# Layer 3's cross-attention values: worked out at layer 2's end instead of beside layer 0's experts

## The chip, the cores and the metric

The kernel runs on one core of a Trainium2 chip. The core has a matrix engine (TensorE, in profiles PE, with its weight loads as PEld), a vector engine (DVE), a scalar engine (ACT), GpSimd (POOL) and a queue processor (SP) that issues most DMAs. Each takes its instructions strictly in order; they meet through semaphores. The metric is the device time of one execution in microseconds, as a median of several.

## The reference, cut to what matters

Four decoder layers, each an attention, a cross-attention to a short context (4 batches of 77 tokens of 128 numbers) and a feed-forward block. The change touches only the preparation of layer 3's cross-attention, whose keys and values come from the context alone:

```
def _L3_xattn_ref(query, key, value, w_q, w_k, w_v, w_o):      # key = value = ctx_1024
    q = (query @ w_q).reshape(B, Q, HEADS, HEAD_DIM).transpose(0, 2, 1, 3)   # 16 heads of 64
    k = (key @ w_k).reshape(B, Kl, HEADS, HEAD_DIM).transpose(0, 2, 1, 3)
    v = (value @ w_v).reshape(B, Kl, HEADS, HEAD_DIM).transpose(0, 2, 1, 3)
    attn = jax.nn.softmax(jnp.einsum('bhqd,bhkd->bhqk', q, k) * scale, axis=-1)
    out = jnp.einsum('bhqk,bhkd->bhqd', attn, v)
    return out.transpose(0, 2, 1, 3).reshape(B, Q, HEADS * HEAD_DIM) @ w_o
...
x = x + _L2_ffn_ref(_layernorm(x), ...)
x = x + _L3_attn_ref(_layernorm(x), Wq, Wk, Wv)     # softmax over the batch axis, then a causal mask
x = x + _L3_xattn_ref(_layernorm(x), ctx_1024, ctx_1024, w_q, w_k, w_v, w_o)
```

Since `attn @ (v_h @ w_o_h)` equals `(attn @ v_h) @ w_o_h`, the kernel multiplies each head's values with its rows of `w_o` ahead of time: a table of 16 heads x 77 tokens x 4 batches x 128 numbers, called `vo`.

## The kernel before, in words

**Tiling.** Activations lie as x, 16 tiles of 128 tokens by 128 numbers (4 tiles a batch), and transposed as xT (128 by 2048). Everything is in float32. A matmul of 128 by 128 weights with 512 columns appears in the profile as two records. Matmul results go to eight banks of PSUM, which are dealt out under tags: `f`, `acc` and `s` while expert blocks run, `mm` (7) and `s` (1) from layer 2's feed-forward block to the end of layer 3's attention.

**Order.** The program is written as Python generators. `weave(dense, chain, every, lead)` takes steps of a dense stream and puts a step of a chain in after every `every` steps; `turns` alternates streams. A scheduler then orders each engine's instructions by that priority and by what it reckons to be ready. On the chip the order is fixed: an instruction that waits holds up all behind it on its engine.

**Stage A (345 to 472 us).** The dense stream is `ffn("l0_ffn", second, ...)`, layer 0's experts for batches 2 and 3 (two matmuls gate and up into banks `f`, an activation on ACT at L1029, one product with up and one with the routing weight c on DVE, a down matmul into `acc` at L1037), in turns with `l3_context`. The chain is layer 1's attention and cross-attention for batches 0 and 1 and the routing of layer 1's experts (`route`): two norms, transposes (L516), the context softmax (POOL's reduction, L536, turned at L543), the sigmoid (L585), the choice of 8 experts on DVE, the turned weights (L666), a store of these to DRAM and the load of c (L989). The next weave has layer 1's experts as its dense stream: two shared units a batch that need no c, then routed ones that do. At most five units can wait for c (tile `h` has five buffers, `f` four banks).

`l3_context` (L2079) runs over eight head pairs hp. For each: a matmul for keys (weights w_k, 128 columns) and a copy `x3kT` by ACT, stored to DRAM (`x3_k`); a matmul for values (w_v) and a copy `x3vT`; after a yield, eight matmuls of 77 rows with w_o (two heads, four batches), two copies `x3vo` by ACT and one store to DRAM (`x3_vo`).

**Stage B (1878 to 1980 us).** Layer 2's feed-forward ends with `l2_dense(b)` for each batch (residual, norm, two dense matmuls through bank `s`, norm, and the layer's closing norm). `l3_keys` then fills `kb` and `vo` from DRAM: a memset by POOL and loads by SP. Beside `dense(3)` runs layer 3's attention: `project(b)` (q, k, v of a batch), `three()` (scores and exps of the first three batches), then `project(3)` and `fourth()` (the last batch's scores, the rescaling of all four on DVE and POOL) and `close(b)`. `l3_xattn` comes after it; it reads `kb` from its second step and `vo` in its step `values`, from 1991 us on.

**Weights.** `want(i)` loads packs of the list `feed` into four slots in turn; `pack` returns them. A load waits until the slot's earlier weights are used up. `load` takes a pack into a pool of its own.

Of the kernel before, what the change touches and what calls it, by code (L numbers as in the profile page):

```python
# [13 lines left out]
F32 = mybir.dt.float32  # L14
# [8 lines left out]
P = 128  # L23
B, S, D = 4, 512, 128
NT = B * S // P
TB = S // P
L = 77
# [264 lines left out]
class Net:  # L292
# [1786 lines left out]
    def l3_context(self, pool):  # L2079

        nc = self.nc
        Wk, Wv, Wo = (self.load("l3_xattn." + n, pool, "x3" + n) for n in "kvo")
        kd = self.away.tile([2, 64, 8, B, L], F32, name="x3_k")
        vd = self.away.tile([16 * L, B, D], F32, name="x3_vo")
        self.x3 = kd, vd
        yield
        for hp in range(8):
            c = slice(hp * P, hp * P + P)
            pk = self.bank("f", (P, B, L))
            self.dot(pk.rearrange("p b l -> p (b l)"), (Wk["k"][:, c], self.const["ctxT"]))  # L2090
            k = pool.tile([P, B, L], F32, tag="x3kT", name="x3kT", bufs=2)
            nc.scalar.copy(k, pk)
            for h in range(2):
                nc.sync.dma_start(kd[h, :, hp], k[64 * h : 64 * h + 64])
            pv = self.bank("f", (P, B * L))
            self.dot(pv, (Wv["v"][:, c], self.const["ctxT"]))
            vT = pool.tile([P, B * L], F32, tag="x3vT", name="x3vT", bufs=2)
            nc.scalar.copy(vT, pv)
            yield
            vo = pool.tile([L, 2, B, D], F32, tag="x3vo", name="x3vo", bufs=2)  # L2100
            for h in range(2):
                po = self.bank("f", (P, B, D))
                r = slice(64 * h, 64 * h + 64)
                for b in range(B):
                    self.dot(po[:L, b, :], (vT[r, b * L : b * L + L], Wo["o"][r, c]))
                nc.scalar.copy(vo[:, h], po[:L])
            nc.sync.dma_start(vd[2 * hp * L : 2 * (hp + 1) * L].rearrange("(h l) b d -> l h b d", l=L), vo)
            yield

    def l3_keys(self, pool):  # L2110


        kd, vd = self.x3
        kb = pool.tile([P, 8, B, 2, L], F32, name="kb")
        n, rest = 16 * L // P, 16 * L % P
        vo = pool.tile([P, n + 1, B, D], F32, name="vo")
        self.nc.gpsimd.memset(kb, 0.0)
        for h in range(2):
            self.nc.sync.dma_start(kb[64 * h : 64 * h + 64, :, :, h, :], kd[h])
        self.nc.sync.dma_start(vo[:, :n], vd[: n * P].rearrange("(r p) b d -> p r b d", p=P))  # L2120
        self.nc.sync.dma_start(vo[:rest, n], vd[n * P :])
        self.x3 = kb, vo

    def l3_xattn(self, base, pool):

# [78 lines left out]
def chained(*chains):  # L2204
    for c in chains:
        yield from c


def some(steps, n):

    for _ in range(n):
        if next(steps, steps) is steps:
            return
        yield


def build(nc, packs, dram):
    first, second = GROUPS
    of = lambda stage: [n for n in packs if n.startswith(stage + ".") and n[-1].isdigit()]
    f2 = [f"l2_ffn.{kind}{hp}" for hp in range(8) for kind in ("qkv", "o")]  # L2220
    feed = ["l0_attn.qk", "l0_attn.vo"]
    at = {}
    for name, part in (
        ("l0a", of("l0_ffn")), ("l0b", of("l0_ffn")), ("l1a", of("l1_ffn")), ("l1b", of("l1_ffn")),
        ("l2", f2 + f2), ("x3", ["l3_xattn.q"]), ("l3", of("l3_ffn")[:3]),
    ):
        at[name] = len(feed)
        feed += part
    with tile.TileContext(nc) as tc, ExitStack() as ctx:
        net = Net(ctx, tc, packs, dram, feed)  # L2230
# [3 lines left out]
        def open_pool(name, right=False):  # L2234
            pools[name] = ExitStack()
            return pools[name].enter_context(net.pool(name, right=right))

        close_pool = lambda name: pools.pop(name).close()
# [31 lines left out]
        s2 = open_pool("s2", right=True)  # L2270
        w2 = net.load("s2", s2, "w")

        def chain2(group):
            yield from both(group, lambda b: chained(net.l1_attn(b, w2, s2), net.l1_xattn(b, w2, s2)))
            yield from net.route("l1_ffn", group, w2, s2)
# [1 line left out]
        x3c = open_pool("x3c")  # L2277
        net.weave(
            net.turns(net.ffn("l0_ffn", second, 16, at["l0b"], ff), net.l3_context(x3c)),
            chained(net.l1_context(s2, w2), chain2(first)), 0.48, 3,  # L2280
        )
        close_pool("x3c")
        net.weave(net.ffn("l1_ffn", first, 64, at["l1a"], ff), chain2(second), 0.97, 3)
# [26 lines left out]
        f2 = open_pool("f2")  # L2310
# [15 lines left out]
        dense = lambda b, fast=False: net.l2_dense(b, y[b], w4, s4, fast)  # L2326
# [2 lines left out]
        close_pool("f2")  # L2329


        net.l3_keys(open_pool("x3c"))
        a3 = open_pool("a3")
        net.want(at["x3"])
        project, three, fourth, close = net.l3_attn(w4, a3)
        net.weave(dense(3, fast=True), chained(project(0), project(1), project(2), three()), 1.15)
        net.weave(chained(project(3), fourth()))
        net.weave(chained(*[close(b) for b in range(B)]), net.norm(0), 1, 1)
        close_pool("a3")
        close_pool("s4")  # L2340
        close_pool("gates")

# [2 lines left out]
        x3 = open_pool("x3")  # L2345
# [38 lines left out]
        dense = net.ffn("l3_ffn", (3,), 32, at["l3"], ff, net.spread3)  # L2384
# [31 lines left out]
```

## Time and profile before

| what | value |
|---|---|
| median of 4 runs | 2236.36 us (2231.95 to 2237.71) |
| profiled execution: device time, span | 2243.5 us, 2241.7 us |
| PE busy | 2102.8 us (94%), 8980 matmul records |
| DVE, ACT, POOL busy | 1606.3 (72%), 998.2 (45%), 555.6 us (25%) |
| first and last `x3vo` copy (ACT) | 349.9 and 446.7 us, 16 copies of 0.58 us |
| `vo` loads issued | 1874.1 and 1883.6 us (2304 and 160 KB) |
| first and last read of `vo` (L2189) | 1991.0 and 2122.6 us |
| mean DMA rate | 96 GB/s |

The profile is of one execution, which ran 7 us above the median; sums against its rows are made against its own span. Busy times of PE are those of pipelined records and overlap by up to 0.17 us at each change of group, so start times are the better measure of what a matmul costs. "Idle before" names the engine and line whose signal ended a wait. Granted clock is TensorE's, 1.00 at full speed.

### The profile page before, as it was taken

Reading aid. Unit: us, or ns where it says so; the run is one execution under the profiler, and the core shown is the slowest. Engines: PE = TensorE matmul, PEld = TensorE weight load, DVE = VectorE, ACT = ScalarE, POOL = GpSimd, SP = SyncE. Lnnn points to the kernel's source line nnn. Section 1 sums busy time; section 2 is a strip of 40 time slices with the busy share of each in tenths; the row PEclk is TensorE's granted clock in tenths of the full one; section 3 lists DMA queues with packets and bytes.
Section 4 is the critical chain, followed back from the end, with each engine's and each line's share of the span. In section 5 each row is a group of like instructions: output and inputs, shape, how many; then the busy total and the mean of one; then the engine's idle time right before and its main releaser. Section 6 shows DMA issues by size and latency. Waiting matters only on the chain.

```text
span 2241.7 us, 28186 instructions
## 1 busy us (share of the span) xinstructions
PE 2102.8 (94%) x8980; PEld 1114.1 (50%) x8980; DVE 1606.3 (72%) x4061; ACT 998.2 (45%) x2044; POOL 555.6 (25%) x695
## 2 busy tenths in 40 slices
PE   6999899999999999899999999999999999499887
PEld 3556555645544554445444544444444444366553
DVE  7676576476675768778977788776776774688735
ACT  4565545543434554434543454343433344356531
POOL 1000000000000000433333333333333331335733
PEclk8998899999999999999999999999999999799988
DMA  6321144154344342333443444443444344111122
GB/s 169 94 72 44 34 115 121 61 127 117 104 129 113 84 122 78 104 85 101 106 116 96 106 117 120 122 120 105 115 112 107 94 112 102 57 39 34 31 73 78
DMA packets 89811, 214.93 MB, mean 96 GB/s; under 512 B 21970, under 2 KB 40850, under 8 KB 89406
## 3 DMA queue, kind: packets, MB, share of 16 engines
q1 hardware_dynamic: 86094, 209.20, 35.0%
q0 software_dynamic: 3568, 3.93, 0.6%
q8 instruction: 71, 1.16, 0.2%
q14 instruction: 78, 0.64, 0.1%
HBM read 184.00 MB, written 23.53 MB: 93 GB/s over the span
## 4 chain that ended last, share of the span: by engine, by line
PE 73%; DVE 16%; issue 4%; ACT 3%; POOL 2%; DMA 1%; SPq 0%; another core or an unknown queue 0%; DVEq 0%; POOLq 0%; ACTq 0%
PE mm L426 20%; PE f L426 13%; PE mm L1878 8%; PE s L426 8%; PE acc L1037 6%; PE mm L1850 5%; PE mm L1825 4%; DVE h L437 2%; PE mm L1160 1%; PE mm L1227 1%; DVE m L1167 1%; PE mm L1205 1%; DVE at_m L1907 1%; PE acc L2189 1%; PE s L516 1%
## 5 line engine op out<-in xcount | busy, mean ns | idle before, releaser
L1786 POOL TENSOR_TENSOR gvx<-gvx 128x512 f32<-128x512 f32 (+1 forms) x256 | 260.4, 1017 | 551.2 <-DVE gvx L437 482.7
L426 PE MATMUL f<-xT,w_l_ffn 128*128 128x512 f32 (+1 forms) x700 | 338.1, 605 | 1.2 <-ACT h L1029 0.7
L1909 ACT ACTIVATE at_e<-mm,at_m 128x512 f32<-128x512 f32 x256 | 173.0, 685 | 294.2 <-DVE at_m L1907 275.5
L426 PE MATMUL mm<-w_l_ffn_qkv,xT 128*128 128x512 f32 x512 | 267.0, 606 | 4.2 <-ACT at_e L1909 1.7
L1878 PE MATMUL mm<-og,w_l_ffn_o 128*128 128x512 f32 x512 | 265.2, 602 | 1.4 <-DVE og L437 1.4
L437 DVE TENSOR_TENSOR h<-h,f 128x512 f32<-128x512 f32 (+1 forms) x192 | 131.1, 684 | 142.8 <-PE f L426 103.7
L1029 ACT ACTIVATE h<-f 128x512 f32<-128x512 f32 x189 | 112.4, 596 | 240.4 <-PE f L426 200.4
L1037 PE MATMUL acc<-h,w_l_ffn 128*128 128x512 f32 x378 | 196.7, 604 | 6.8 <-DVE h L437 6.2
L426 PEld LDWEIGHTS f<-xT,w_l_ffn 128*128 128x128 f32 (+1 forms) x700 | 126.9, 192 | 132.9 <-issue 112.0
L437 DVE TENSOR_TENSOR gvx<-mm,gv 128x512 f32<-128x512 f32 x256 | 174.5, 683 | 22.4 <-PE mm L426 18.6
L437 DVE TENSOR_TENSOR og<-mm,c 128x512 f32<-128x512 f32 x256 | 173.9, 681 | 18.3 <-PE mm L1878 16.1
L1826 ACT COPY eT<-mm 128x512 f32<-128x512 f32 x256 | 137.6, 596 | 83.4 <-PE mm L1825 83.2
L1907 DVE TENSOR_REDUCE at_m<-mm 128x1 f32<-128x512 f32 x256 | 161.0, 681 | 11.9 <-PE mm L426 10.5
L1825 PEld LDWEIGHTS mm<-ident,at_e 128*128 128x128 f32 x1024 | 120.8, 142 | 68.1 <-issue 47.6
L1878 PEld LDWEIGHTS mm<-og,w_l_ffn_o 128*128 128x128 f32 x512 | 91.8, 191 | 112.2 <-issue 91.0
L1825 PE MATMUL mm<-ident,at_e 128*128 128x128 f32 x1024 | 136.2, 275 | 5.3 <-ACT at_e L1909 5.3
L426 PEld LDWEIGHTS mm<-w_l_ffn_qkv,xT 128*128 128x128 f32 x512 | 87.6, 191 | 95.1 <-issue 59.0
L426 PE MATMUL mm<-roped 64*128 64x512 f32 x512 | 130.9, 622 | 1.7 <-DVE roped L437 1.1
L1167 DVE TENSOR_REDUCE m<-mm 128x1 f32<-128x512 f32 (+3 forms) x176 | 104.9, 635 | 34.9 <-PE mm L1163 34.0
L1850 PE MATMUL mm<-eT,v 128*64 128x512 f32 x512 | 118.6, 599 | 0.0
L1037 PEld LDWEIGHTS acc<-h,w_l_ffn 128*128 128x128 f32 x378 | 70.9, 192 | 91.8 <-issue 61.6
L437 DVE TENSOR_TENSOR h<-h,c 128x512 f32<-128x512 f32 x160 | 110.4, 695 | 3.7 <-DMA c<-l_ffn_w 0.9
(458 smaller groups left out, 3557.1 us busy)
## 6 DMA issues: line engine op xcount, KB each, us to landing
c<-gates SPq DMA_DIRECT2D x256, 256.0 KB
c<-l_ffn_w SPq DMA_DIRECT2D x96, 384.0 KB
w_l_ffn<-in_l_ffn SPq DMA_DIRECT2D x26, 576.0 KB
w_l_ffn_qkv<-in_l_ffn_qkv SPq DMA_DIRECT2D x16, 640.0 KB
w_l_ffn_o<-in_l_ffn_o SPq DMA_DIRECT2D x16, 512.0 KB
rot<-qk SPq DMA_DIRECT2D x128, 64.0 KB
d<-inverted SPq DMA_DIRECT2D x64, 128.0 KB
k_parts<-k SPq DMA_DIRECT2D x12, 384.0 KB
```

Of the source, the lines that this page charges most:

```text
L426: self.nc.tensor.matmul(out, lhsT=lhsT, rhs=rhs, start=i == 0, stop=i == len(pairs) - 1)
L437: self.nc.vector.tensor_tensor(out, a, b, op)
L1029: nc.scalar.activation(h, pg, AF.Silu)
L1037: nc.tensor.matmul(acc["t"], lhsT=W["d" + u], rhs=h, start=i == 0, stop=i == n - 1)
L1167: nc.vector.tensor_reduce(m[:, i, h0 : h0 + per], ps, AX.X, ALU.max, negate=True)
L1786: nc.gpsimd.tensor_tensor(x[:, :, :m], x[:, :, :m], x[:, :, m : 2 * m], ALU.add)
L1825: nc.tensor.transpose(p[:, j, :], es[i][hl][:, j * P : j * P + P], self.ident)
L1826: nc.scalar.copy(eT[hl][:, :, i * P : i * P + P], p)
L1850: nc.tensor.matmul(po[64 * hl : 64 * hl + 64, :], lhsT=m["v"][:, j, hl, :], rhs=eT[hl][:, j, :], start=j == 0, stop=j == TB - 1,)
L1878: nc.tensor.matmul(acc, lhsT=W["o"][:, (e - 1) * D : e * D], rhs=hs.pop(e - 1), start=e == 1, stop=e == E)
L1907: nc.vector.tensor_reduce(m, s, AX.X, ALU.max, negate=True)
L1909: nc.scalar.activation(e[:, :n], s, AF.Exp, bias=m, accum_out=den)
```

## The change

Three things change. The value part of `l3_context` becomes a generator of its own, `l3_values`, with the same work per head pair; the key part stays where it is, with one yield a pair instead of two. `l3_values` takes w_v and w_o from the slots (two packs new in `feed`, ahead of the query weights) and banks `mm` instead of `f`. It is woven in at stage B: eight of its sixteen steps in turns with `dense(3)`, the rest in turns with `project(3)` and `fourth()`; the reload of `vo` moves from `l3_keys` to a function that is called after both. Two weaving rates are changed with it, 0.48 to 0.36 and 1.15 to 1.8.

```
--- before.py
+++ after.py
@@ -2079,7 +2079,7 @@
     def l3_context(self, pool):
 
         nc = self.nc
-        Wk, Wv, Wo = (self.load("l3_xattn." + n, pool, "x3" + n) for n in "kvo")
+        Wk = self.load("l3_xattn.k", pool, "x3k")
         kd = self.away.tile([2, 64, 8, B, L], F32, name="x3_k")
         vd = self.away.tile([16 * L, B, D], F32, name="x3_vo")
         self.x3 = kd, vd
@@ -2092,14 +2092,24 @@
             nc.scalar.copy(k, pk)
             for h in range(2):
                 nc.sync.dma_start(kd[h, :, hp], k[64 * h : 64 * h + 64])
-            pv = self.bank("f", (P, B * L))
+            yield
+
+    def l3_values(self, base, pool):
+
+        nc = self.nc
+        Wv, Wo = (self.pack(base + i, "l3_xattn." + n) for i, n in enumerate("vo"))
+        vd = self.x3[1]
+        yield
+        for hp in range(8):
+            c = slice(hp * P, hp * P + P)
+            pv = self.mm()[:, : B * L]
             self.dot(pv, (Wv["v"][:, c], self.const["ctxT"]))
             vT = pool.tile([P, B * L], F32, tag="x3vT", name="x3vT", bufs=2)
             nc.scalar.copy(vT, pv)
             yield
             vo = pool.tile([L, 2, B, D], F32, tag="x3vo", name="x3vo", bufs=2)
             for h in range(2):
-                po = self.bank("f", (P, B, D))
+                po = self.mm((P, B, D))
                 r = slice(64 * h, 64 * h + 64)
                 for b in range(B):
                     self.dot(po[:L, b, :], (vT[r, b * L : b * L + L], Wo["o"][r, c]))
@@ -2109,17 +2119,20 @@
 
     def l3_keys(self, pool):
 
-
-        kd, vd = self.x3
+        kd, self.vd = self.x3
         kb = pool.tile([P, 8, B, 2, L], F32, name="kb")
-        n, rest = 16 * L // P, 16 * L % P
-        vo = pool.tile([P, n + 1, B, D], F32, name="vo")
+        vo = pool.tile([P, 16 * L // P + 1, B, D], F32, name="vo")
         self.nc.gpsimd.memset(kb, 0.0)
         for h in range(2):
             self.nc.sync.dma_start(kb[64 * h : 64 * h + 64, :, :, h, :], kd[h])
-        self.nc.sync.dma_start(vo[:, :n], vd[: n * P].rearrange("(r p) b d -> p r b d", p=P))
-        self.nc.sync.dma_start(vo[:rest, n], vd[n * P :])
         self.x3 = kb, vo
+
+    def l3_values_back(self):
+
+        vo = self.x3[1]
+        n, rest = 16 * L // P, 16 * L % P
+        self.nc.sync.dma_start(vo[:, :n], self.vd[: n * P].rearrange("(r p) b d -> p r b d", p=P))
+        self.nc.sync.dma_start(vo[:rest, n], self.vd[n * P :])
 
     def l3_xattn(self, base, pool):
 
@@ -2222,7 +2235,7 @@
     at = {}
     for name, part in (
         ("l0a", of("l0_ffn")), ("l0b", of("l0_ffn")), ("l1a", of("l1_ffn")), ("l1b", of("l1_ffn")),
-        ("l2", f2 + f2), ("x3", ["l3_xattn.q"]), ("l3", of("l3_ffn")[:3]),
+        ("l2", f2 + f2), ("x3v", ["l3_xattn.v", "l3_xattn.o"]), ("x3", ["l3_xattn.q"]), ("l3", of("l3_ffn")[:3]),
     ):
         at[name] = len(feed)
         feed += part
@@ -2277,7 +2290,7 @@
         x3c = open_pool("x3c")
         net.weave(
             net.turns(net.ffn("l0_ffn", second, 16, at["l0b"], ff), net.l3_context(x3c)),
-            chained(net.l1_context(s2, w2), chain2(first)), 0.48, 3,
+            chained(net.l1_context(s2, w2), chain2(first)), 0.36, 3,
         )
         close_pool("x3c")
         net.weave(net.ffn("l1_ffn", first, 64, at["l1a"], ff), chain2(second), 0.97, 3)
@@ -2329,14 +2342,19 @@
         close_pool("f2")
 
 
+        x3v = open_pool("x3v", right=True)
+        values = net.l3_values(at["x3v"], x3v)
+        next(values)
         net.l3_keys(open_pool("x3c"))
         a3 = open_pool("a3")
         net.want(at["x3"])
         project, three, fourth, close = net.l3_attn(w4, a3)
-        net.weave(dense(3, fast=True), chained(project(0), project(1), project(2), three()), 1.15)
-        net.weave(chained(project(3), fourth()))
+        net.weave(net.turns(dense(3, fast=True), some(values, 8)), chained(project(0), project(1), project(2), three()), 1.8)
+        net.weave(net.turns(chained(project(3), fourth()), values))
+        net.l3_values_back()
         net.weave(chained(*[close(b) for b in range(B)]), net.norm(0), 1, 1)
         close_pool("a3")
+        close_pool("x3v")
         close_pool("s4")
         close_pool("gates")
```

## The prediction

> **What bounds the kernel now.** The chain of waits comes first: 73% of what ended last is TensorE (PE), 16% VectorE (DVE). The slices say where it is not: PE is at 9 nearly everywhere, with a 4 in the 35th slice (1905 to 1961 us). The table by stretch then takes the two stages that the change touches.
>
> ```profile
> PE 73%; DVE 16%; issue 4%; ACT 3%; POOL 2%; DMA 1%; SPq 0%; another core or an unknown queue 0%; DVEq 0%; POOLq 0%; ACTq 0%
> ...
> 345.00:472.00 127.00, 124.69 (x573) 76.11 (x571) 78.22 (x305) 64.38 (x120) 8.67 (x12) 0.97 0.36 98
> ...
> 1878.00:1906.00 28.00, 24.82 (x91) 15.99 (x90) 15.80 (x72) 11.67 (x24) 3.06 (x4) 0.88 0.54 114
> ...
> 1919.00:1932.50 13.50, 0.66 (x4) 0.42 (x4) 9.02 (x46) 2.72 (x7) 0.07 (x1) 0.63 0.02 1
> 1932.50:1940.00 7.50, 6.77 (x23) 4.84 (x24) 0.00 (x0) 2.93 (x7) 0.00 (x0) 0.52 0.00 0
> 1940.00:1970.00 30.00, 14.10 (x91) 12.35 (x90) 26.78 (x37) 4.12 (x9) 16.92 (x28) 0.77 0.44 176
> ```
>
> After the stretch and its length come the busy times of PE, weight load, DVE, ACT, POOL, then the granted clock. Stage A, 345 to 472, where the values are made now, has 2.3 us of idle PE in 127. Stage B, 1878 to 1980, where they go, has 13 us of it before 1932.5 and 16 us after 1940. The diff thus looks like a plain gain. Two more views decide whether it is: what paces each stage once PE is not it, and where in B the new instructions stand. The timeline of both stages gives the first, the instruction order of the two builds the second.
>
> ```profile
> 345.61 0.68 PE L426 MATMUL f<-w_const,w_l_xattn_v 128*128 128x308 f32 x2
> 358.50 1.60 PE L426 MATMUL f<-w_l_xattn_o,x3vT 64*77 64x128 f32 x16
> 410.88 1.32 PE L543 MATMUL s<-ident,sm_e 128*77 128x128 f32 x8 [1.04 <-POOL sm_e L536]
> 440.81 0.60 ACT L585 ACTIVATE sig<-s 128x512 f32<-128x512 f32 x1
> 462.24 1.06 PE L666 MATMUL s<-ident,w_halves 128*64 128x128 f32 x8
> 471.81 2.96 DVE L437 TENSOR_TENSOR h<-h,c 128x512 f32<-128x512 f32 x3 [0.87 <-DMA c<-l_ffn_w]
> 1932.55 1.64 PE L516 MATMUL s<-ident,xn 128*128 128x128 f32 x4 [12.42 <-ACT xn L492]
> 1934.86 2.07 PE L426 MATMUL mm<-xT,w_s 128*128 128x512 f32 x2 [0.68 <-ACT xT L517]
> 1939.97 2.32 PE L426 MATMUL mm<-q,k 128*128 128x512 f32 x8
> 1941.04 1.21 DVE L437 TENSOR_TENSOR top<-mm,m 128x512 f32<-128x512 f32 x2 [8.88 <-PE mm L426]
> 1956.65 0.79 PE L426 MATMUL mm<-v,e 128*128 128x128 f32 x2 [14.36 <-POOL e L2057]
> ```
>
> In A the last steps of layer 1's chain (softmax turned at L543, router's sigmoid, weights turned at L666, c back from DRAM) are a serial line that ends in units that wait for c. In B the idle time is one serial line too: layer 2's dense block for the last batch, its projection, the last batch's scores, then DVE and POOL up to the first matmul on e.
>
> **The moved work.** Each head pair has one 308-column matmul (records start 0.26 us apart, so 0.52) and eight of 77 rows (chain of waits: 20 records in 3.44, less four 512-wide ones at 0.43, leaves 16 in 1.72). That is 2.24 us of PE, eight times: 17.9. With it go 8 ACT copies of 0.42 and 16 of 0.58 (12.6 us), 8 stores to DRAM and two weight loads.
>
> **Stage A gives back less than 17.9.** Both builds stop at the same place: 64 gate and up matmuls and 27 down matmuls after the previous routing (counted from the order), blocked until c comes. So the gain is how much earlier c comes, not how much PE is freed. Step by step:
> - Up to L543 the scheduler fills the holes with dense work: 16 more 512-wide matmuls (13.8 us) for 12.2 us of values (net of two key matmuls done sooner). PE reaches the chain's steps 1.6 later; 1.0 of that was waiting for POOL. +0.5.
> - From L543 to the residual add (425.3) PE has only the chain's small matmuls in both: 0.
> - Two layer norms: four DVE products (2.7 us) leave that stretch, but each chain of small operations is serial: -1.3. PE, with its dense work used up, idles there. One gate matmul now stands between the router's two halves at a low clock (a pair at 419.01 took 2.07 instead of 1.02), and its activation and the 1.28 us table load stand ahead of the sigmoid on ACT: +0.1. Sigmoid in sum: -0.7.
> - Sigmoid to L666 is 20.8 us now. The routing's own DVE steps and POOL's copy add up to 14.9 by their starts; six products at 0.62 stay between them, plus 0.4 of hops: 19.2. -1.6. L666 in sum -2.3.
> - c lands 9.6 us after L666 as now. Two products fewer there and a norm that starts sooner win about 1.5; ACT loads tables 8 times instead of 4 in the stretch that follows (1.28 each), half of which PE sees through late activations: +1.5 or so.
>
> A comes to -2.3. Bounds: -17.9 if PE bounds the stage throughout; +3 if nothing is won and half of the extra loads (2.6) and 0.5 are lost. I stand near the second, since rows pace the chain in all but its first part.
>
> **Stage B pays for it.** The order shows none of the eight pairs in the 12.42 us hole: PE takes its instructions in order, and the transposes of xn stand ahead of what follows. Four pairs are before that hole, four behind it, among the last batch's projection and scores.
> - Pairs 0 to 2, from 1880 to 1897: 5.6 us put before batch 2's transposes, 2.5 us of them in an idle gap (1892.8 to 1895.3). ACT's copies stand before its normalize: 1.0 late. The last batch's dense block absorbs most of it, because PE catches up while DVE does the norm: +0.2 at its d_s (1906.4).
> - Four d_s matmuls alternate with ACT's relu through one bank, 1.9 us a turn. Two copies of 0.58 and exps now ahead of them on ACT make the last relu end at about 1917.4 instead of 1914.9: +2.3.
> - Behind the hole pairs 4 and 5 put 2.76 us (two 0.52, one 1.72) ahead of the first score, which DVE waits for. The clock rises by time, not by work (1.87 us for the first 0.86), so it is not doubled: +2.75.
> - Pairs 5 to 7 stand between the scores; DVE then has 27 us of work in 30, so they hide. POOL gets 4.3 us of memsets and casts between its 512- and 384-wide blocks, and 2.7 of idle absorb most: +0.5.
>
> In sum +5.8. Bounds: +2.5 if only the pairs ahead of the score count, less their overlap; +10 if copies on ACT (pairs 4 to 7: 6.3 us) stall the exps as well.
>
> **DMA and queues.** On SP the load of w_o waits for pass 30's last matmul (1845); the two c loads behind it wait for DVE until 1850 anyway, as do inverted, d and the q weights behind those, so 0. The eight stores and the 2304 KB reload stand last but for the gate bias, slots and back: the last store is issued about 1956 (the first score then starts near 1945, the copies of pairs 5 to 7 take 11 us more), the reload (some 250 GB/s from 1878 to 1892 with the keys) lands about 1970, and its first reader is at 1991. Cover 20 us; without it each us counts in full. kb, behind the first store, arrives some 12 us later but is read at 1983. Slots and back follow; nothing reads them before 2040.
>
> **Sum.** -2.3 + 5.8 = +3.5 against the profiled span of 2241.7 (device time 2243.5, 7.1 above the median of 2236.4): span 2245.2, median 2239.9.
>
> The Trainium skill (TensorE: Matmul & The Clock Gate, "What's actually happening") says that an idle window of 3.4 us halves the clock and as much busy time restores it, which speaks against freeing PE in A. The row in B took 4.4 us to recover. By the rule A's new gap of about 4 us costs up to 1.7 more (half of 3.4), giving +5.2; by the rows it is +3.5.
>
> **Rivals.**
> - *The copies decide (slower).* Place: ACT in B, from the relus to the last exp. Price: relus +2.3, the score +2.75, and 3 of the 6.3 us of copies before exps that DVE waits for: +8, and A gives 0: 2244.4. It decides once DVE shows waits for ACT's e or f after the first score. For it: DVE is at 90% there, so any wait counts. Against: by starts the exps are ahead of need.
> - *PE sets A (faster).* If the chain keeps up, half the 17.9 comes back (-9) and B costs +5: 2232.4. For it: 124.69 of 127 busy. Against: dense work runs out at the hq step, and DVE and POOL rows fill 410 to 472.
> - *It does what it says.* A -17.9, B +5.8: -12, 2224.3. For it: the idle sum in B. Against: the order.
>
> **How the numbers follow.** About 0.2% (4.5 us) is what a measurement tells from no change. Forecast (0 to +7, centre +3.5) 0.50: slower 0.22, within 0.28. Copies 0.22, all slower. PE sets A 0.20: half faster, half within. As it says 0.08, faster. Sum: faster 0.18, within 0.38, slower 0.44. The range leaves out 0.1 at each end: 2230.5 to 2248; the forecast's own is 2236 to 2243.5.
>
> **What would show it.** Right: PE idle of 14 us or more between 410 and 472 (2.3 now), L666 2 us earlier, the hole before xn's transposes still 12 us, the first score 4 to 6 us later against the last layer-2 matmul, no wait for vo. Wrong: L666 over 6 us earlier, a filled hole, or DVE idle between the scores.

## The result, and the profile after

The changed kernel takes 2244.2 us (median of 50 runs, 2236.7 to 2255.9) against 2238.4 for the kernel before (76 runs beside them): a ratio of 1.0025, 95% interval 1.0016 to 1.0033, or 5.6 us. A second comparison, in a later set of runs, gave 1.0037 (1.0018 to 1.0057). The forecast was +3.5. In absolute terms 2244.2 lies 4.3 above the forecast's centre of 2239.9; 2.0 of that is the kernel before, which came out above the median of its first four runs.

One execution alone doesn't show this: the profiled run after has a span of 2240.9 us, less than the 2241.7 before. The start, which the change doesn't touch, varies more than that: from the first instruction to the first matmul with w_k it takes 345.1 and 337.3 us in two profiles of the kernel before. So the two are compared by stretches, from landmark to landmark, with two profiles of each kernel:

| stretch, us | before | after | difference |
|---|---|---|---|
| start to the first w_k matmul | 345.1, 337.3 | 338.5, 342.9 | by chance |
| from there to L543 | 65.8, 66.8 | 65.1, 65.1 | -1.2 |
| L543 to the sigmoid | 29.9, 29.9 | 30.0, 27.7 | -1.1 |
| sigmoid to L666 | 21.4, 21.4 | 19.1, 18.6 | -2.6 |
| L666 to the first product with the new c | 9.6, 9.6 | 9.9, 9.6 | +0.2 |
| from there to layer 2's last matmul (L1878) | 1414.3, 1414.3 | 1412.8, 1416.4 | +0.3 |
| **stage A in sum: first w_k to last L1878** | 1541.0, 1542.0 | 1536.9, 1537.3 | **-4.4** |
| last L1878 to d_s of the last batch | 20.3, 20.4 | 22.7, 22.7 | +2.3 |
| d_s to y, the block's result (L1955) | 12.3, 12.3 | 13.7, 13.7 | +1.4 |
| y to the first read of a last-batch score by DVE | 22.4, 22.4 | 25.1, 25.1 | +2.7 |
| from there to the first xattn_q matmul | 39.0, 39.0 | 42.4, 42.4 | +3.5 |
| **stage B in sum: last L1878 to xattn_q** | 93.9, 94.0 | 103.9, 103.9 | **+10.0** |

Here d_s and y are tiles of layer 2's dense block for the last batch: the input of its two matmuls and its result. -4.4 and +10.0 make +5.6, what the runs show. Stage B repeats to a tenth of a microsecond; stage A doesn't, for a reason below. Five of the experiments (e1 to e4 and e7) have the changed kernel's order in stage A, but for a matmul or two at its end; with them there are seven profiles of it, from 1533.2 to 1537.3 with a mean of 1535.4, so stage A's gain is nearer 6 than 4.4. The sum is then +3.9, and the two comparisons gave 5.6 and 8.2: that the table meets the first so exactly is chance.

Stage A after, by stretch (length; busy PE, weight load, DVE, ACT, POOL; granted clock) and on the timeline (start, us, engine, line):

```profile
345.00:472.00 127.00, 114.44 (x437) 67.46 (x435) 80.33 (x307) 58.81 (x107) 11.29 (x14) 0.89 0.32 79
410.00:472.00 62.00, 50.15 (x171) 30.06 (x171) 37.69 (x156) 22.85 (x40) 3.46 (x4) 0.78 0.28 65
```

```profile
404.72 0.66 PE L543 MATMUL s<-ident,sm_e 128*77 128x128 f32 x4 [0.45 <-POOL sm_e L536]
433.61 0.60 ACT L585 ACTIVATE sig<-s 128x512 f32<-128x512 f32 x1
452.73 1.07 PE L666 MATMUL s<-ident,w_halves 128*64 128x128 f32 x8 [2.52 <-POOL w_halves L659]
462.65 3.07 DVE L437 TENSOR_TENSOR h<-h,c 128x512 f32<-128x512 f32 x3 [2.55 <-DMA c<-l_ffn_w]
465.47 4.16 PE L1037 MATMUL acc<-h,w_l_ffn 128*128 128x512 f32 x6
```

PE is now idle for 11.9 of the 62 us in which the chain ends (2.1 before), L666 waits for POOL (2.52) and the first product with the new c for its load (2.55): the chain sets the pace, not PE. Only 4.4 of the 17.9 us of freed PE time come back, 6 by the mean of seven profiles. The price is in the clock, 0.78 against 0.94, and in the last line: six down matmuls take 0.69 each instead of 0.51.

Stage B after, timeline:

```profile
1887.53 0.33 PE L516 MATMUL s<-ident,xn 128*128 128x128 f32 x1
1887.79 0.44 PE L426 MATMUL mm<-w_l_xattn_o,x3vT 64*77 64x128 f32 x2
1888.16 0.33 PE L516 MATMUL s<-ident,xn 128*128 128x128 f32 x1
1888.42 0.44 PE L426 MATMUL mm<-w_l_xattn_o,x3vT 64*77 64x128 f32 x2
1888.79 0.33 PE L516 MATMUL s<-ident,xn 128*128 128x128 f32 x1
...
1890.42 0.66 PE L457 MATMUL s<-ident,y 128*128 128x128 f32 x4
1891.11 0.69 DVE L437 TENSOR_TENSOR d_z<-xn,s 128x512 f32<-128x512 f32 x1 [7.57 <-PE s L457]
...
1925.75 1.63 PE L516 MATMUL s<-ident,xn 128*128 128x128 f32 x4 [12.43 <-ACT xn L492]
1929.93 1.23 PE L426 MATMUL mm<-w_const,w_l_xattn_v 128*128 128x308 f32 x2
1932.81 1.60 PE L426 MATMUL mm<-w_l_xattn_o,x3vT 64*77 64x128 f32 x16
1936.92 0.69 DVE L437 TENSOR_TENSOR top<-mm,m 128x512 f32<-128x512 f32 x1 [11.75 <-PE mm L426]
1951.94 0.80 PE L426 MATMUL mm<-v,e 128*128 128x128 f32 x2 [6.21 <-POOL e L2057]
```

The 12.4 us hole is still there and empty (before 12.42, now 12.43), with pairs on both sides of it. Ahead of it a pair's matmuls alternate with batch 2's transposes; behind those stand the transposes of the last batch's y (at L457 still the sum that enters its dense block), for which DVE waits 7.57 us. In the kernel before the same place reads:

```profile
1895.28 1.63 PE L516 MATMUL s<-ident,xn 128*128 128x128 f32 x4 [2.50 <-ACT xn L492]
1897.59 1.11 PE L457 MATMUL s<-ident,y 128*128 128x128 f32 x4 [0.68 <-ACT xT L517]
1898.74 0.69 DVE L437 TENSOR_TENSOR d_z<-xn,s 128x512 f32<-128x512 f32 x1 [4.04 <-PE s L457]
```

The last part of stage B is on GpSimd. After (POOL, with DVE's product among it):

```profile
1951.84 0.86 POOL L376 DMA_DIRECT2D w_s_gate<-in_s_gate  x1
1952.93 0.97 POOL L819 MEMSET none<- 128x1040 f32 x1
1954.37 0.94 POOL L820 MEMSET none<- 128x1024 f32 x1
1954.76 4.72 DVE L437 TENSOR_TENSOR e<-e,f 128x384 f32<-128x384 f32 x1
1955.27 1.88 POOL L817 CAST pick<-own_rows 96x2048 bf16<-96x2048 f32 x1
1957.12 1.94 POOL L2051 TENSOR_TENSOR e<-e,f 128x384 f32<-128x384 f32 x2
```

Before, the cast, the DVE step beside it and DVE's product:

```profile
1942.22 1.89 POOL L817 CAST pick<-own_rows 96x2048 bf16<-96x2048 f32 x1
1942.75 1.90 DVE L437 TENSOR_TENSOR f<-m,top 128x512 f32<-128x512 f32 x1
1959.41 1.35 DVE L437 TENSOR_TENSOR e<-e,f 128x384 f32<-128x384 f32 x1
```

The constants for layer 3's slots (memsets, own_rows, pick) ran at 1940 to 1944 before, ahead of the first block's products, where the cast stretched one step of DVE's, f<-m,top, to 1.90 us (0.68 after, at 1938.25). In the new order they stand behind the 512-wide block; what made the scheduler put them there was not settled. POOL's 384-wide products wait for them, and DVE's own product of 384 columns takes 4.72 us instead of 1.35: it ends 0.4 us after POOL's second product. The Trainium skill (SBUF — State Buffer, "Who interferes with whom") has a rule for this: a DVE instruction with two inputs in SBUF contends with a GpSimd instruction that reads SBUF, not with one that only writes it. The rows agree: pick and the two products read. A DVE product of the same width beside a memset took 0.54 (f<-f,r at 1953.78), beside POOL's two products alone 1.35.

### The profile page after: what moved, and what is told of

It is laid out like the page before. It is cut to its first block, busy times and chain, and to the rows that moved or that the text cites. A ratio compares the mean times of both kernels' runs of the same rounds, so it can differ in the third digit from the quotient of the medians.

```text
span 2240.9 us, 28202 instructions
## 1 busy us (share of the span) xinstructions
PE 2099.7 (94%) x8980; PEld 1116.0 (50%) x8980; DVE 1607.6 (72%) x4061; ACT 1001.3 (45%) x2048; POOL 554.9 (25%) x695
## 5 line engine op out<-in xcount | busy, mean ns | idle before, releaser
L1878 PE MATMUL mm<-og,w_l_ffn_o 128*128 128x512 f32 x512 | 265.7, 603 | 1.4 <-DVE og L437 1.4
L1907 DVE TENSOR_REDUCE at_m<-mm 128x1 f32<-128x512 f32 x256 | 161.0, 681 | 11.9 <-PE mm L426 10.5
L1878 PEld LDWEIGHTS mm<-og,w_l_ffn_o 128*128 128x128 f32 x512 | 91.8, 191 | 112.1 <-issue 91.4
L492 ACT ACTIVATE xn<-x,nmr,rstd 128x128 f32<-128x128 f32 x192 | 80.2, 484 | 80.3 <-DVE nmr L490 69.9
```

The costliest lines, as they stand in the source:

```text
L1878: nc.tensor.matmul(acc, lhsT=W["o"][:, (e - 1) * D : e * D], rhs=hs.pop(e - 1), start=e == 1, stop=e == E)
L1907: nc.vector.tensor_reduce(m, s, AX.X, ALU.max, negate=True)
```

## The experiments

All runs by stretch (us, one profile each; before, after and the last row two). A stands for the way from the first w_k matmul, B for that from the last L1878 matmul; ratios are to the kernel before in the same set of runs, five rounds each for the experiments, the changed kernel's own first.

| run | A to c | A to last L1878 | B to y | B to first score | B to xattn_q | ratio (95%) |
|---|---|---|---|---|---|---|
| before | 126.7, 127.8 | 1541.0, 1542.0 | 32.6 | 55.0 | 93.9, 94.0 | 1 |
| after | 124.1, 120.9 | 1536.9, 1537.3 | 36.4 | 61.5 | 103.9 | 1.0025 (1.0016 to 1.0033); 1.0037 (1.0018 to 1.0057) |
| e1 no values | 121.8 | 1533.5 | 32.9 | 55.5 | 94.4 | 0.9985 (0.9969 to 1.0000) |
| e2 POOL last | 123.0 | 1535.2 | 36.4 | 61.5 | 101.4 | 1.0005 (0.9989 to 1.0021) |
| e3 none before | 121.0 | 1536.7 | 32.8 | 58.0 | 103.8 | 1.0005 (0.9985 to 1.0024) |
| e4 in the hole | 121.6 | 1533.2 | 33.4 | 59.6 | 98.9 | 0.9995 (0.9978 to 1.0011) |
| e5 late in A | 130.4 | 1549.0 | 32.5 | 54.9 | 93.8 | 1.0049 (1.0032 to 1.0066) |
| e7 in the hole 2 | 123.0 | 1534.9 | 33.4 | 55.6 | 94.3 | 0.9981 (0.9961 to 1.0001) |
| e8, e10 late in A, ahead | 121.8, 123.8 | 1531.4, 1537.1 | 32.9, 32.6 | 55.3, 55.0 | 94.3, 94.0 | 0.9973 (0.9950 to 0.9995); 0.9979 (0.9965 to 0.9993) |

**e1, the values left out: what A alone is worth.**

```
...
-        net.weave(net.turns(dense(3, fast=True), some(values, 8)), chained(project(0), project(1), project(2), three()), 1.8)
-        net.weave(net.turns(chained(project(3), fourth()), values))
+        net.weave(dense(3, fast=True), chained(project(0), project(1), project(2), three()), 1.15)
+        net.weave(chained(project(3), fourth()))
```

> The changed kernel without the values' work anywhere: no matmuls with w_v and w_o, no copies, no stores; vo is filled from the rows of x instead (the same 2464 KB), so the output is another. This leaves stage A as the change made it and stage B as it was before. Theory (A gives little, B takes all of it back): about 3 us under the kernel before, ratio 0.9986, all of it between 345 and 570 us; the way from the last layer-2 matmul (L1878) to the first xattn_q matmul as before, 93 us within 1. Rival (PE sets A, so the freed 17.9 us count): 9 or more under, ratio 0.996 or less. Rival (freeing PE in A is itself a loss, by its clock and the extra table loads): ratio 1.000 or more.

Measured: 3.4 us under the kernel before by the ratio, and B back at 94.4. So by the medians the freed 17.9 us are worth a fifth of themselves, and freeing them is no loss. The size is not sharp: the interval of the ratio holds 0 to 7 us, and the stretches put it at 7 to 8 in this one profile (A 7.5 to 8.6 less, B 0.5 more).

**e2, GpSimd in the program's order.**

```
+        with tc.manual_schedule(engines={mybir.EngineType.Pool}):
+            net.weave(net.turns(chained(project(3), fourth()), values))
...
+            net.empty_slots(s5)
```

> The changed kernel with GpSimd's instructions from the last batch's scores on in the order of the program: the constants for the slots (memsets, own_rows, the cast pick, 5.3 us with the gate's load), which the change put between the 512- and the 384-wide blocks of the last batch's weights, then come after all four blocks. All other engines' order up to the first matmul on e is the same. Theory (these constants, not the copies or PE, cost 4 us there): 3 to 4 us under the changed kernel, about 1.001 of the kernel before, and the DVE product e<-e,f of 384 columns takes 1.4 us again, not 4.7. Rival (PE's and ACT's work between the scores costs them): no change, 1.0025, and the way from the first score to xattn_q stays at 44 us.

Measured: 1.0005, and 2.5 of stage B's 10 us gone. The same DVE product, and POOL's beside it:

```profile
1954.26 2.51 POOL L2051 TENSOR_TENSOR e<-e,f 128x384 f32<-128x384 f32 x2 [2.51 <-DVE f L437]
1954.57 1.35 DVE L437 TENSOR_TENSOR e<-e,f 128x384 f32<-128x384 f32 x1
```

4.72 is 1.35 again and POOL waits for DVE. From the first score to xattn_q it is 39.9, against 42.4 after and 39.0 before. The theory's 3 to 4 us were 2.5. The last 1.0 of the 3.5 is left; the pairs between the scores stand there, but no run tells them from the rest.

**e3, no pair ahead of the hole.**

```
-        net.weave(net.turns(dense(3, fast=True), some(values, 8)), chained(project(0), project(1), project(2), three()), 1.8)
+        net.weave(dense(3, fast=True), chained(project(0), project(1), project(2), three()), 1.15)
```

> The changed kernel with no head pair beside the last dense block: all sixteen steps go in turns with the last batch's projection and scores, and the rate there is 1.15 as before. In the order of the build two pairs then stand ahead of the first score, two between the first scores, and four after them; the slots' constants come after GpSimd's blocks. Theory (the pairs ahead of the hole cost 4.3 by standing before the transposes of batch 2, the two ahead of the score 2.4, those behind it little): about 1 us over the kernel before, ratio 1.0005, and d_s of the last batch 20 us after the last L1878 matmul as before. Rival (the copies on ACT decide: 12.6 us of them now stand among the exps): 5 or more over the changed kernel's own +5.6, ratio 1.005.

Measured: y at 32.8 again, 3.6 us back, so the pairs ahead of the hole are what cost there. The first score is 3.0 late by the two pairs ahead of it. But B in sum is 103.8: the theory took the four pairs behind the scores for nearly free, and they aren't. PE:

```profile
1946.78 1.60 PE L426 MATMUL mm<-w_l_xattn_o,x3vT 64*77 64x128 f32 x16 [0.56 <-ACT x3vT L2108]
1952.02 1.74 PE L426 MATMUL mm<-w_l_xattn_o,x3vT 64*77 64x128 f32 x16 [2.92 <-ACT x3vT L2108]
1955.65 2.92 PE L426 MATMUL mm<-w_l_xattn_o,x3vT 64*77 64x128 f32 x16 [0.56 <-ACT x3vT L2108]
1960.45 2.92 PE L426 MATMUL mm<-w_l_xattn_o,x3vT 64*77 64x128 f32 x16 [0.56 <-ACT x3vT L2108]
1963.31 0.79 PE L426 MATMUL mm<-v,e 128*128 128x128 f32 x2
```

In each pair PE waits for ACT's copy between the w_v matmul and those with w_o; once behind an exp for 2.92 us. Then the clock falls to half, and a pair takes 4.8 us. The matmuls on e stand behind them on PE until 1963, 26.4 us after the first score instead of 15.6. The rival, ACT, is right about the wait but not about who bears it: it is PE, not the exps. The ratio shows none of this price: it is 1.0005, +1.1 us, where the stretches make +5, which its interval (to +5.4) just holds. Where the rest went wasn't settled; the readings within B, which repeats to a tenth between profiles of one kernel, don't hang on it.

**e4, pairs in the hole.** Ten steps beside the dense block, from its thirteenth step on, six behind the third score, GpSimd as in e2.

```
+        within = some(values, 10)
+
+        def beside(steps, at, per):
+            for n, _ in enumerate(steps):
+                yield
+                if n >= at:
+                    yield from some(within, per)
+
+        net.weave(beside(dense(3, fast=True), 12, 2), chained(project(0), project(1), project(2), three()), 1.15)
+        with tc.manual_schedule(engines={mybir.EngineType.Pool}):
+            four = fourth()
+            net.weave(chained(project(3), some(four, 4), values, four))
...
```

> The changed kernel with the head pairs put where PE is idle: ten steps only after the last dense block's second layer norm has begun (a hole of 12.4 us, five pairs are 11.2), six behind the third of the last batch's scores, and GpSimd's slot constants last. Theory (the place costs, not the work): stage B within 1.5 us of before, stage A's 3 us kept, so 2 under the kernel before, ratio 0.999. Rival (the work costs wherever it stands, by the copies on ACT or by the clock): B +5 or more, ratio 1.001 or more.

Measured: 0.9995, between the theory's 0.999 and the rival's 1.001; B is 5.0 over before, which is the rival's number. The timeline names two things that the theory missed:

```profile
1921.58 2.44 PE L426 MATMUL mm<-w_l_xattn_o,x3vT 64*77 64x128 f32 x16 [2.56 <-ACT x3vT L2108]
1925.91 2.92 PE L426 MATMUL mm<-w_l_xattn_o,x3vT 64*77 64x128 f32 x16 [0.56 <-ACT x3vT L2108]
1929.35 1.65 ACT L492 ACTIVATE xn<-x,nmr,rstd 128x128 f32<-128x128 f32 x4
1929.90 1.63 PE L516 MATMUL s<-ident,xn 128*128 128x128 f32 x4 [1.07 <-ACT xn L492]
```

The last pairs again wait for ACT's copies and run at half clock, and ACT's normalize, whose input was ready at 1927.0, stands behind their copies until 1929.35. Besides, the scores of the first three batches had slid behind the pairs on PE, so that DVE did them inside the last norm.

**e7, the same with both mended.** The three batches' scores placed ahead of the pairs, four pairs a side, w_v's matmul a pair ahead.

```
+        d3, fore = dense(3, fast=True), chained(project(0), project(1), project(2), three())
+        net.weave(some(d3, 12), fore, 1.15)
+        net.weave(d3, some(values, 5), 0.6)
+        with tc.manual_schedule(engines={mybir.EngineType.Pool}):
+            four = fourth()
+            net.weave(chained(project(3), some(four, 4), values, four))
...
+        ahead = first(0)
         for hp in range(8):
+            vT, ahead = ahead, first(hp + 1) if hp < 7 else None
```

> Like the run with the pairs in the hole, with three changes: the scores of the first three batches are placed ahead of the pairs in the program (there they stood behind, so DVE did them inside the last norms); four pairs in place of five and a half go beside the end of the last dense block, the other four behind the third of the last batch's scores; and each pair's w_v matmul is issued a pair ahead, so that PE does not wait for ACT's copy between it and the w_o matmuls. GpSimd's constants come last. Theory (the place costs, not the work): xattn_q at most 96 us after the last L1878 matmul (93.9 before, 98.9 in the earlier run, 103.9 in the changed kernel), c at 121 to 124 us, so 2 to 5 us under the kernel before, ratio 0.998 to 0.999. Rival (the pairs cost about 5 us wherever they stand in stage B, by the half clock): xattn_q at 98 or more, ratio 0.9995 or more.

Measured: xattn_q at 94.3 and 0.9981.

```profile
1912.61 1.60 PE L426 MATMUL mm<-w_l_xattn_o,x3vT 64*77 64x128 f32 x16
1914.86 1.60 PE L426 MATMUL mm<-w_l_xattn_o,x3vT 64*77 64x128 f32 x16
1921.77 1.63 PE L516 MATMUL s<-ident,xn 128*128 128x128 f32 x4 [5.32 <-ACT xn L492]
```

The pairs no longer wait, and of the hole 5.32 us are left. All eight pairs stand in stage B and cost 0.3 us there, 9.6 us less than where the change put them. Of the 9.6, e2 gives 2.5 to GpSimd's order alone; from there to e4 it is another 2.5, and from e4 to here 4.6 for three edits at once, which no run separates.

**e5, the values late in A.** From the kernel before: the values' part made a generator and woven into the last 19 of the chain's 65 steps (the routing is the last 13).

```
...
-            chained(net.l1_context(s2, w2), chain2(first)), 0.48, 3,
+            chained(net.l1_context(s2, w2), beside(chain2(first), 46, 1)), 0.48, 3,
```

> The kernel before with the values kept in stage A, but as a generator of their own that is woven into the end of the chain (from the second norm before the routing on) instead of in turns with layer 0's experts: PE makes one or two pairs around the turned softmax (L543) and the rest while DVE chooses the experts; units that need no c move behind L666, into the time in which c is under way. Stage B and the rates are those of the kernel before. Theory (in A the work is free where the routing's serial chain leaves PE idle; what the change won there is only that the chain is no longer held up): c as early as in the changed kernel (121 to 124 us after the first key matmul, 126.7 before), no price in B, so 3 to 4 us under the kernel before, ratio 0.9985. Rival (PE sets A: 17.9 us of work must cost there): c at 126 or later, ratio 1.000. Rival (freeing PE in A costs by the clock): c earlier than 121 and the clock in the stretch from 410 to 472 at 0.9 or more, ratio under 0.998.

Measured: 1.0049, c at 130.4, so none of the three was right; the first rival's c of 126 or later came, its ratio of 1.000 did not. The windows, the timeline of PE and DVE's wait for it:

```profile
430.00:440.00 10.00, 8.88 (x38) 6.48 (x39) 9.62 (x44) 3.16 (x6) 0.27 (x1) 0.50 0.16 49
440.00:450.00 10.00, 8.88 (x40) 6.48 (x39) 2.51 (x6) 3.16 (x6) 0.79 (x2) 0.50 0.22 73
```

```profile
442.44 1.39 PE L426 MATMUL f<-w_const,w_l_xattn_v 128*128 128x308 f32 x2
444.39 2.92 PE L426 MATMUL f<-w_l_xattn_o,x3vT 64*77 64x128 f32 x16 [0.56 <-ACT x3vT L2107]
447.25 1.39 PE L426 MATMUL f<-w_const,w_l_xattn_v 128*128 128x308 f32 x2
449.20 2.92 PE L426 MATMUL f<-w_l_xattn_o,x3vT 64*77 64x128 f32 x16 [0.56 <-ACT x3vT L2107]
452.05 1.91 PE L666 MATMUL s<-ident,w_halves 128*64 128x128 f32 x8
453.15 0.68 DVE L432 COPY w_turned<-s 64x512 f32<-64x512 f32 x1 [10.47 <-PE s L666]
```

The granted clock is 0.5 from 425 to 456 us although PE is busy for 89% of the 20 us shown. A pair takes 4.8 us, and L666 stands behind five of them: after L666 DVE continues from an idle time of 10.5 us. POOL's copy w_halves, which L666 reads, ended at 443.4, so the routing itself was early and L666 waited 8.7 us in PE's order. At the 2.24 us a pair takes at full clock, the five would have been done by about 439 (an estimate from 428.07).

**e8 and e10, the same with w_v's matmul a pair ahead** (the edit of e7's last lines, on e5).

> Like the run with the values late in stage A, where a pair took 4.8 us instead of 2.2 because the granted clock stayed at half from 425 to 456 us and PE waited 0.56 us in every pair for ACT's copy; here each pair's w_v matmul is issued a pair ahead, so that PE has no such wait, and the order of the build then has layer 1's first units ahead of L666 again. Theory 1 (the waits and the chain's gaps keep the clock down): clock 0.9 or more between 425 and 456, w_o's sixteen records of a pair in 1.6 us, c at 122 to 124 us after the first key matmul, ratio 0.9985 to 1.000. Theory 2 (matmuls of 64 by 77 do not raise the clock, however close they stand): clock still 0.5 there, 2.9 us for the sixteen records, c at 128 or later, ratio 1.003 or more.

> The kernel with the values late in stage A and w_v's matmuls a pair ahead, once more, for a narrower interval beside the changed kernel. Theory (the routing's idle time in A holds the work at full clock, nothing moves to B): 4 to 7 us under the kernel before, ratio 0.997 to 0.9982, and 7 to 12 us under the changed kernel. Rival (its first run was one chip's luck): ratio 1.000 within 0.0015.

```profile
420.00:430.00 10.00, 10.00 (x75) 7.37 (x73) 6.54 (x42) 6.04 (x15) 0.00 (x0) 1.00 0.20 63
430.00:440.00 10.00, 10.00 (x92) 8.26 (x92) 3.37 (x13) 8.11 (x16) 0.00 (x0) 1.00 0.34 109
```

The clock is at full, sixteen records of w_o take 1.60 us, a pair 2.24, the first product with c comes at 121.8 and 123.8. These are theory 1's numbers, and the ratio is lower than it said; with the 0.56 us of waiting gone, the same small matmuls ran at full clock. They found it full, though: it was so from 418.7 us (417.4 in e10), ahead of all pairs but the first, while in e5 it fell at 425, after a wait of 1.10. So these runs show that such matmuls hold full clock when nothing interrupts them, not that they raise it from half. The order differs in one more thing, layer 1's first units, which stand ahead of L666 here and behind it in e5; they come after the pairs, but before the first product with c, which follows L666 by 13.1 us in e5 and by 9.5 and 9.7 here. Stretch A is 12 to 18 us shorter than in e5, from one matmul's place in a loop and the order that the scheduler made of it; 7 to 9 of that are won by the first product with c. Twice under the kernel before, by 4.7 to 6 us, and 13 us under the changed kernel in the one set that has both (2217.4 against 2230.9), this version beats both kernels, with the values where they were before, only later.

**e6 and e9, both kernels once more**, for a second profile of each; e9 ran beside e10.

> The kernel before, once more, for a second profile. If the difference in stage A is the program's and not that of one execution, c lands 126 to 128 us after the first key matmul again (126.7), against 121.0 to 124.1 in the five profiles with the values away from there, and xattn_q starts 94 us after the last L1878 matmul (93.9).

> The changed kernel once more, on one chip with the next run. By the sum of its parts: stage A 4 to 7 us less, from the first key matmul to the last L1878 matmul (1541 to 1542 in the two profiles of the kernel before), and 103.9 us again from there to xattn_q (93.9 before), so 3 to 6 us over the kernel before, ratio 1.0015 to 1.0027. If stage B's price were that of one execution, the 103.9 would not come back.

Measured: both as expected by stretches (127.8 and 94.0; 1537.3 and 103.9); e6's one run took 2238.5 us. e9's ratio, 1.0037, is above the 1.0015 to 1.0027 that was written down; its interval reaches down to 1.0018.

Of the two rates, 0.48 to 0.36 moves nothing that these runs could show: the changed kernel built with 0.48 has the same order on PE, ACT, POOL and SP, and differs on DVE alone. It wasn't run. 1.8 back to 1.15 with the pairs in place would change the order; it wasn't run either.

## Why the prediction was right, point by point

- **That the two stages nearly cancel, with B the larger: right.** Both terms were too small: A -4.4 for -2.3, B +10.0 for +5.8. The errors took 2.1 of 4.2 off each other, and the sum came out at +5.6 for +3.5: that it came so near is in part luck. B lies at the upper end of its bounds (+10), A well inside.
- **A, to L543: +0.5, measured -1.2.** The step held that more dense work ahead delays PE by 1.6, of which 1.0 was a wait for POOL. In fact the chain came earlier. This step failed; which instruction gained the time wasn't pursued.
- **A, L543 to the sigmoid: -1.2 (the -0.7 is the sum with the step above), measured -1.1; routing: -1.6, measured -2.6.** The mechanism, DVE's products leaving the chain's way and the chain then pacing itself, is what the wait of L666 on POOL shows. The routing's gain was taken over a third too small. L666 came 4.9 us earlier, where 2 was the sign of being right and over 6 that of being wrong. The first of the listed signs, 14 us or more of idle PE between 410 and 472, didn't quite come: 11.9 and 12.1 (the 2.3 beside it is the idle time of all of stage A before; in 410 to 472 it was 2.1).
- **A, c's way unchanged, then -1.5 and +1.5: measured +0.2 and +0.3.** The two terms behind c were not separated. The eight table loads for four came, between L666 and 500 us.
- **The clock in A.** From L543 to the sigmoid, half-clock stretches take 17 us in one profile after and 10 in the other, 6.8 before; the stretch is 30.0 in the one and 27.7 in the other. All seven profiles of this order fall in line: where the first half-clock stretch behind L543 lasts 3.4 us, the way to the sigmoid takes 27.6 to 27.7 (the second profile after, e1, e3, e4), where it lasts 6.8, 29.3 to 30.0 (the first, e2, e7). So the new gaps do cost something by the clock, about 2 us in the worse case, and that is one reason why A doesn't repeat as B does. The rule's 1.7 more was not too much for the first profile, but it comes on top of a larger gain; that its +5.2 lies nearer the measured +5.6 than the +3.5 is no proof of it.
- **B, pairs 0 to 2: +0.2 at d_s, measured +2.3 (2.8 with the half microsecond by which the last L1878 matmul is itself late).** This step failed. It said that the last batch's block absorbs the delay because PE catches up while DVE does the norm. But y's transposes stand on PE behind batch 2's, and the block's chain on DVE starts from them; DVE's wait grew from 4.04 to 7.57. Counted from the last L1878 matmul, batch 2's transposes start 2.9 us late, where the step had 1.0, the block's first DVE step (d_z) 3.0 late and its d_s 2.3: PE catches up some 0.6, not most of it. What PE catches up later doesn't help a chain that starts late. e3 shows it: without those pairs d_s and y are back.
- **B, the relus: +2.3, measured +1.4.** Right in kind: two copies x3vo stand between the relus, whose last one ends 9.9 us after d_s instead of 8.5.
- **B, two pairs ahead of the first score: +2.75, measured +2.7.** The best of the terms.
- **B, POOL: +0.5, measured 3.5 for all behind the first score, of which e2 takes 2.5 away.** The step saw the constants move between the blocks and let 2.7 us of idle time absorb them. It counted POOL's time only, not what they do to DVE, which was at 90% there.
- **No wait for vo and the hole kept at 12 us came as listed; the first score, 4 to 6 us late on the list, was 6.5 late.** The first read of vo comes 11.6 us after xattn_q as before (11.1), and waits for ACT and issue, not for the load.
- **The rival of ACT's copies** gave +8 for A at 0 and B +8. DVE's waits after the first score are for PE (0.36) and for POOL (0.82), none for ACT's e or f; so not by this mechanism. Its sum, +8, lies about as far from the measured +5.6 as the forecast's +3.5, which by itself decides nothing.

## What to carry to other kernels

Moving work from a stage whose busy sum is full to one whose busy sum has a hole pays only where the order puts it in the hole and nothing waits there: here the same eight pairs cost 10 us, 5 us or 0.3 us in the same stage by their place, their own waits and what other engines' orders became (2.5 of the 10 was GpSimd's), and the work looks alike in the busy sums. Before moving, ask what paces the stage they leave: if a serial chain does, the work can stay, later, in the chain's own idle time. And give PE independent matmuls to issue between producer and consumer: with a wait of half a microsecond in every turn its clock stayed at half for 30.7 us here, and without it it stayed full.

## What the hardware showed that was not expected

- At half clock PE didn't recover in 30.7 us with records covering 89% of the time (e5), and didn't drop in 20 us with records, the same small matmuls among them, covering all of it (e8). The Trainium skill (TensorE: Matmul & The Clock Gate, "What's actually happening") says that one sustained busy window of about 3.4 us restores the clock; e5 agrees only if windows with 0.56 us of waiting in each 4.8 don't count as busy. Whether it is the share or the pause that counts stays open.
- Half-clock stretches in all these profiles last 3.4 us or a multiple of it (but for the one that the end cuts short), and some single ones come and go at the same place between executions of one kernel (one at 557 to 564 us in both profiles before and one of the two after). From the first product with c to the last L1878 matmul, the kernels with the changed order in stage A take 1411.6 to 1412.8 us in the five profiles with four half-clock windows of 3.4 us between 500 and 1870 us, and 1415.7 and 1416.4 in the two with seven: some 1.3 us each (an estimate from these), the size of effect that this case is about, and the other reason why A doesn't repeat.
- The last stage, from xattn_q to the end, takes 260.8 to 265.0 us in eight profiles and 245.7 to 246.3 in the four of the sets in which the kernel before ran at 2221.6 and 2221.8 us (e7 to e10; 2238.4 to 2239.2 in the others). These 16 us are nearly the whole difference between the sets. Its cause wasn't looked for; it is why ratios here are taken within a set only.
